# Three moves in the order of a relational graph layer: a maximum's transposes, one pair's input, two gathers of gate rows

## The chip, the cores and the metric

The kernel runs on one core of a Trainium2 chip. The metric is the device time of one execution in microseconds, as the median of several runs. The profile is of one further execution, taken by the hardware profiler; its times are counted from the first instruction.

The core's engines are TensorE (PE; PEld is its weight load), VectorE (DVE), ScalarE (ACT), GpSimd (POOL) and SyncE (SP). Each works through its own instructions in program order. SP, ACT and POOL also issue DMAs. L204 is line 204 of the kernel.

## The reference

One pre-normed graph layer over 1250 nodes of 1024 features, with 20000 typed edges and 8 relations, all in float32:

```python
h = maximum(layernorm(x), 0)
u = h @ root + bias
for r in range(8):
    mask = (edge_type == r)
    sums = segment_sum(h[src] * mask[:, None], dst, num_segments=1250)
    cnt  = segment_sum(mask, dst, num_segments=1250)
    u = u + (sums / maximum(cnt, 1)[:, None]) @ weight[r]
z = concatenate([u, h], axis=1) @ w_gate + b_gate
out = x + tanh(u) * z + h * (1 - z)
```

## The kernel before, in words

**Matrices before edges.** The kernel multiplies h by each of the eight relation matrices first and gathers rows of the products afterwards. There are eleven matrices in all, numbered 0 to 10: the relations, root (8), the lower half of w_gate (9), and the upper half (10), which multiplies u. The nodes are ten blocks of 128 rows, taken in five pairs: pair i holds blocks i and i + 5. We write (s, i) for the product of matrix s with pair i. There are 55 of them, and their order fixes TensorE's order.

**A product.** One product (`product`, L195) multiplies 256 x 1024 by 1024 x 1024 in seven products of quarters, of four 128-deep steps each. We call these the seven adds, j = 0 to 6, in the order A11, S1, S2, S4, S3, A12, A22. Their left operands lie in `h_op[i]`, seven slices of 512 columns; `transposed` (L174) makes the four A slices by TensorE transposes and copies, `left` (L186) the S slices on VectorE (S1 on L189). Their right operands are the quarters of the matrix and four sums of them that VectorE makes (`make_t1` to `make_t4`, L158 to L172); T4 belongs to A22. An add takes about 3.43 us on TensorE. ScalarE and VectorE take the results out of PSUM: L213, L216, L219, L226 and L234 on ScalarE, L222, L227 and L231 on VectorE. Six PSUM banks are shared.

**Slots.** After each add the kernel calls `between(j)`. This is where all other work is put into the engines' orders: generators are advanced, and whatever stands between two of their `yield`s falls behind that add. We call such a piece a slot and count from the first add of the kernel, or of the stage concerned.

**First stage (products (0,0) to (3,3)).** `norms` normalises the pairs, stores h (`store`, L410) to `h_dram`, transposes it (`factored`), and stores x + h (`with_x`, L414 and L415) to `xh_dram`. `both` is the norm of a pair's two blocks: statistics on VectorE (L388), a square root on ScalarE, and the scaled relu on ScalarE (L405). Pairs 0 and 1 are loaded ahead of the first product. The x tiles come from a pool of three; pair 1's two lie in a part of `h_op[3]` that is not used yet. In `norms`, pair 2 is normalised in slot 8, pair 3 in slot 12, and pair 4 block by block in slots 16 and 18. Beside it, `columns` makes key columns from the edge lists, and later slots count and place the edges in a table and order the nodes by their number of edges.

**Edges.** The relations form three groups, matrices 0 to 2, 3 to 5, and 6 to 7. For each group and each block of nodes, a row of u gathers its edges' rows of the product, one edge per node and slot: an indirect DMA on POOL (L834) into one of four `got` tiles, and a multiply and add on VectorE (L842). Between blocks and groups u lies in `u_dram`, written by L308 and read by L302. The second group's slots, 76 of them, lie beside the products of matrices 6 and 7 (70 adds).

**Passes.** Nodes with more edges than the slots provide need further passes, whose number is computed at run time. `passes_needed` (L901) takes maxima on VectorE (L908 and L910) in its first step and then transposes them on TensorE (L914 and L915). A few small VectorE instructions (L917 to L925) turn them into `n_pass`, which every engine reads before the branch at L974, at the end of the second group. `with_passes` advances this generator once per slot of the second group.

**The gate.** The last matrix runs pair by pair in the order of the sorted nodes. `gate_u` gathers h rows, takes tanh of u and makes the left operand of the next product. `gate_load` loads u (`last_dram`) and gathers root rows (`hr_dram`), added on L1042, for the pair after the next. `gate_rows` gathers rows of `z_dram` and `xh_dram` and multiplies them on L1078. `finish` forms the output. For pair 0 the z rows go to `h_op[2]`; `z_dram` is written by the SP stores of matrix 9 (L277). All gathers are issued by POOL in program order.

Of the kernel before, what the change touches and what calls it, by code (L numbers as in the profile page):

```python
# [9 lines left out]
F32 = mybir.dt.float32  # L10
# [9 lines left out]
def tile_rgcn_highway(  # L20
# [34 lines left out]
    P = 128  # L55
    N, D = x.shape
# [6 lines left out]
    NP = ND // 2  # L63
# [16 lines left out]
    A11, A12, A22, S1, S2, S3, S4 = range(7)  # L80
# [23 lines left out]
    z_dram = dram.tile([N, D], F32, name="z_dram")  # L104
    xh_dram = dram.tile([N, D], F32, name="xh_dram")
# [68 lines left out]
    def transposed(aop, part, of, n):  # L174

        for half, to in enumerate(((A11, A12), (A21, A22))[part]):
            p = bank().rearrange("p (k f) -> p k f", k=KQ)
            for i in range(KQ):
                k = KQ * half + i
                nc.tensor.transpose(p[:, i, :n], of[:n, k * P:(k + 1) * P], ident[:n, :n])  # L180
            copy = nc.vector.tensor_copy if half else nc.scalar.copy
            copy(aop[:, to, :, :n], p[:, :, :n])
            if n < P:
                nc.gpsimd.memset(aop[:, to, :, n:], 0.0)

    def left(aop, part=0):  # L186

        if part != 3:
            nc.vector.tensor_add(aop[:, S1], aop[:, A21], aop[:, A22])  # L189
            nc.vector.tensor_sub(aop[:, S2], aop[:, S1], aop[:, A11])  # L190
        if part != 1:
            nc.vector.tensor_sub(aop[:, S4], aop[:, A12], aop[:, S2])
            nc.vector.tensor_sub(aop[:, S3], aop[:, A11], aop[:, A21])
# [94 lines left out]
    node = const.tile([P, G, ND], I32, name="node")  # L288
# [9 lines left out]
    h_op = [keep.tile([P, 7, KQ, P], F32, name=f"h_op{i}") for i in range(NP)]  # L298

    def rows_of(to, of, at):  # L300

        nc.gpsimd.indirect_dma_start(  # L302
            out=to, out_offset=None, in_=of,
            in_offset=bass.IndirectOffsetOnAxis(ap=at, axis=0))
# [52 lines left out]
    with ExitStack() as early:  # L357
# [4 lines left out]
        xpool = first_part.enter_context(tc.tile_pool(name="xpool", bufs=3))  # L362

        def load_x(i, part, t=None):
            d = i + part * NP
            n = nrows(d)
            if t is None:
                t = xpool.tile([P, D], F32, name="xt")
            nc.sync.dma_start(t[:n], x[d * P:d * P + n, :])
            return t  # L370

        def scratch(i, part):

            return h_op[i][:, 2 * part:2 * part + 2].rearrange("p a k f -> p (a k f)")
# [42 lines left out]
        def both(a, b, parts=1):  # L417

            a.stats(0)
            a.stats(1)  # L420
            a.spread()
            b.stats(0)
            a.scale()
            a.relu(parts)
            b.stats(1)
            b.spread()
            b.scale()
            b.relu(parts)

        def factored(i, blocks):  # L430
            for part in range(2):
                transposed(h_op[i], part, blocks[part].ht, blocks[part].n)
# [7 lines left out]
        x1 = [load_x(1, 0, scratch(NP - 2, 0))]  # L440
        fac[0].load_b21()
        x1.append(load_x(1, 1, scratch(NP - 2, 1)))
        xs = [load_x(2, 0)]


        ix0 = first_part.enter_context(tc.tile_pool(name="ix0", bufs=1))
# [288 lines left out]
        def norms():  # L735
            yield
            yield
            both(*b1)
            fac[0].make_t4()
            for b in b1:  # L740
                b.store()
            yield
            yield
            factored(1, b1)
            left(h_op[1])
            yield
            for b in b0:
                b.with_x()
            xs.extend([load_x(2, 1), load_x(3, 0)])
            yield  # L750
            for b in b1:
                b.with_x()
            yield
            yield
            for i in range(2, NP):
                blocks = []
                if i < NP - 1:
                    blocks = [Normed(i + part * NP, xs.pop(0), scratch(NP - 1, part))
                              for part in range(2)]
                    both(*blocks)  # L760
                    yield
                    for b in blocks:
                        b.store()
                    yield
                    factored(i, blocks)
                    left(h_op[i])
                    yield
                    for b in blocks:
                        b.with_x()
                    xs.append(load_x(i + 1, 1))  # L770
                    if i + 2 < NP:
                        xs.append(load_x(i + 2, 0))
                    yield
                else:
                    for part in range(2):
                        xt = xs.pop(0)
                        b = Normed(i + part * NP, xt, xpool.tile([P, D], F32, name="xt"))
                        b.stats(0)
                        b.stats(1)
                        b.spread()  # L780
                        b.scale()
                        b.relu()
                        b.store()
                        yield
                        transposed(h_op[i], part, b.ht, b.n)
                        b.with_x()
                        yield
                    left(h_op[i])
            first_part.close()

        def index():
# [17 lines left out]
    with ExitStack() as edges_part:  # L809
# [91 lines left out]
        def passes_needed():  # L901

            far_k = small.tile([P, NHI], F32, name="far_k")
            nc.vector.memset(far_k, 0.0)
            for g in range(G):
                for d in range(ND):
                    if K[g][d] < SLOTS:
                        nc.vector.reduce_max(far_k[:, g * ND + d:g * ND + d + 1],  # L908
                                             w_of[:, g, d, K[g][d]:], axis=AX.X)
            nc.vector.reduce_max(most[:, 1:2], far_k, axis=AX.X)  # L910
            for _ in range(3):
                yield
            p = bank()
            nc.tensor.transpose(p[:1, :P], most[:, 0:1], ident)  # L914
            nc.tensor.transpose(p[:1, P:2 * P], most[:, 1:2], ident)  # L915
            top = const.tile([1, 2], F32, name="top")
            nc.vector.reduce_max(top, p[:1, :2 * P].rearrange("o (a b) -> o a b", a=2), axis=AX.X)  # L917
            nc.vector.tensor_scalar(top[:, 0:1], top[:, 0:1], float(MORE - 1 - SLOTS), 0.0,
                                    op0=OP.add, op1=OP.max)
            nc.vector.tensor_single_scalar(top[:, 1:2], top[:, 1:2], 0.0, op=OP.is_gt)  # L920
            top_i = const.tile([1, 2], I32, name="top_i")
            nc.vector.tensor_copy(top_i, top)
            nc.vector.tensor_single_scalar(top_i[:, 0:1], top_i[:, 0:1], 2,
                                           op=OP.arith_shift_right)
            nc.vector.tensor_max(n_pass, top_i[:, 0:1], top_i[:, 1:2])  # L925
# [10 lines left out]
        s, i = next(steps)  # L936
        while s <= R0[1]:
            step(s, i)
            s, i = next(steps)
# [8 lines left out]
        def with_others(e):  # L948
# [6 lines left out]
            for _ in others:  # L955
# [3 lines left out]
        s, i = beside(with_others(edges(0, range(ND), u_back(0))), sum(K[0]) + 1, s, i,  # L959
                      R0[2] - 1)  # L960
# [6 lines left out]
        for g in range(1, G - 1):  # L967
            e = edges(g, range(ND), u_back(g))
            s, i = beside(with_passes(e) if g == G - 2 else e, sum(K[g]) + 1, s, i, R0[g + 2] - 1)
# [4 lines left out]
        with tc.If(passes > 0):  # L974
# [15 lines left out]
            scratch = got()  # L990
# [14 lines left out]
            with tc.For_i(0, passes, 1):  # L1005
# [9 lines left out]
                for c in range(NCH):  # L1015
                    n = nedges(c)
# [13 lines left out]
        LG = G - 1  # L1030
# [17 lines left out]
        def place_of(what, i, part):  # L1048

            o = ("z", "d").index(what)  # L1050
            if i % 2:
                w = fac[NM - 1].spare[o].rearrange("p k n -> p (k n)")
                return w[:, part * D:(part + 1) * D]
            return h_op[2 + o][:, 2 * part:2 * part + 2].rearrange("p a k f -> p (a k f)")

        def pair(i):
            return [(part, 2 * i + part, nrows(2 * i + part)) for part in range(2)]

        hs, xhs, adds, outs = {}, {}, [], []
# [7 lines left out]
        def gate_rows(i, j):  # L1067

            if j == 0:
                for part, d, n in pair(i):  # L1070
                    at = node[:n, LG, d:d + 1]
                    rows_of(place_of("z", i, part)[:n], z_dram[:, :], at)
                    xhs[part] = got()
                    rows_of(xhs[part][:n], xh_dram[:, :], at)
            elif j == (2 if i else 5):
                for part, d, n in pair(i):
                    zt, dt = place_of("z", i, part), place_of("d", i, part)
                    nc.vector.tensor_mul(zt[:n], zt[:n], dt[:n])  # L1078
                    nc.vector.tensor_add(zt[:n], zt[:n], xhs[part][:n])
# [109 lines left out]
```

## Time and profile before

| | us |
|---|---|
| median of 3 runs (lowest, highest) | 1408.04 (1406.12, 1408.88) |
| profiled execution, its own time | 1409.14 |
| its span, first to last instruction | 1407.3 |
| TensorE busy | 1369.7 (97%) |
| VectorE busy | 862.4 (61%) |
| GpSimd busy | 616.8 (44%) |
| ScalarE busy | 339.4 (24%) |
| mean granted TensorE clock | 0.99 |

Busy time counts the instructions of an engine, not its waits. Where an idle time stands in brackets before an instruction, an arrow names what ended it, its releaser. A line of the timeline has a start, a length, the engine, the line of the kernel, the operation, the tiles written and read, and the number of instructions merged into it. DMA-issuing instructions on SP are short; their data moves afterwards.

### The profile page before, as it was taken

The page shows a single profiled execution, that of the slowest core. Times are in us where ns is not written, and L with a number is a line of the kernel's source. Part 1 is how long each engine was busy: PE and PEld are TensorE (multiplying, and loading weights), DVE is VectorE, ACT ScalarE, POOL GpSimd, SP SyncE. Part 2 cuts the span into 40 slices and gives each one's busy share as a digit, 9 for nine tenths or more (in the row PEclk, how much of TensorE's full clock was granted, in tenths as well). Part 3 has the DMA queues.
Part 4 walks back from the last instruction along what each step waited for, and adds up shares of the span by engine and source line. Part 5 has one row for each costly group of instructions (what it writes and reads, how often), then busy time and mean ns, then how long its engine had stood idle before and what let it go on. Part 6 is the DMA issues. An engine that isn't in the chain of part 4 may idle for free.

```text
span 1407.3 us, 11968 instructions
## 1 busy us (share of the span) xinstructions
PE 1369.7 (97%) x3562; PEld 617.4 (44%) x3562; DVE 862.4 (61%) x1658; ACT 339.4 (24%) x721; POOL 616.8 (44%) x567
## 2 busy tenths in 40 slices
PE   7989999999999999999999599999999999999998
PEld 4444444444444444444444244444444444444443
DVE  7755866886767834455456545654446565465985
ACT  3235655565521111011111010111111111121220
POOL 0001655665561634665664434544426433422641
PEclk9999999999999999999999899999999999999999
DMA  9653766675544257269677725787659844556761
GB/s 327 219 191 114 182 119 129 151 194 103 123 134 134 63 180 195 88 199 269 209 279 252 273 89 196 275 305 261 231 171 328 304 161 171 190 188 207 255 234 56
DMA packets 109863, 272.73 MB, mean 194 GB/s; under 512 B 25890, under 2 KB 27920, under 8 KB 109664
## 3 DMA queue, kind: packets, MB, share of 16 engines
q0 software_dynamic: 48864, 128.60, 28.4%
q1 hardware_dynamic: 39808, 101.38, 24.7%
q10 hardware_dynamic: 21120, 41.95, 9.6%
q8 instruction: 28, 0.46, 0.1%
q14 instruction: 43, 0.35, 0.1%
HBM read 214.20 MB, written 80.65 MB: 210 GB/s over the span
## 4 chain that ended last, share of the span: by engine, by line
PE 72%; issue 9%; DMA 6%; POOL 5%; DVE 2%; ACT 0%; POOLq 0%; DVEq 0%; ACTq 0%
PE ps L204 71%; DMA got<-y,idx 3%; DMA node_dram<-ids,pos_i 2%; POOL got L834 2%; POOL got L302 1%; POOL out_dram L308 1%; DMA got<-hr_dram,node 1%; PE ps_n L585 1%; DVE u L842 1%; DMA got<-h_dram,node 1%; POOL u_dram L308 1%; PE ps L180 0%; POOL idx L302 0%; POOL h_op L302 0%; DMA xh_dram<-xt 0%
## 5 line engine op out<-in xcount | busy, mean ns | idle before, releaser
L204 PE MATMUL ps<-w,h_op 128*128 128x512 f32 x3080 | 1347.5, 596 | 2.9 <-DVE h_op L189 2.9
L204 PEld LDWEIGHTS ps<-w,h_op 128*128 128x128 f32 x3080 | 580.3, 191 | 700.3 <-issue 691.9
L842 DVE SCALAR_TENSOR_TENSOR u<-got,w_of,u 128x1024 f32<-128x1024 f32 (+1 forms) x192 | 246.2, 1283 | 197.3 <-DMA got<-y,idx 189.2
L834 POOL DMA_INDIRECT got<-y,idx x202 | 244.8, 1212 | 243.1 <-DVE u L842 163.4
L664 POOL DMA_INDIRECT table<-row_col,at_i x157 | 179.3, 1142 | 159.1 <-DVE at_i L660 65.7
L222 DVE TENSOR_TENSOR row<-row,ps 128x512 f32<-128x512 f32 x55 | 37.7, 685 | 113.3 <-PE ps L204 86.3
L226 ACT COPY part<-ps 128x512 f32<-128x512 f32 x55 | 32.2, 586 | 291.2 <-PE ps L204 282.6
L234 ACT COPY row<-ps 128x512 f32<-128x512 f32 x50 | 29.3, 585 | 253.1 <-PE ps L204 253.1
L213 ACT COPY row<-ps 128x512 f32<-128x512 f32 x55 | 32.1, 585 | 165.0 <-PE ps L204 148.5
L227 DVE TENSOR_TENSOR row<-row,part 128x512 f32<-128x512 f32 x55 | 37.8, 688 | 50.4 <-ACT part L226 44.2
L216 ACT COPY row<-ps 128x512 f32<-128x512 f32 x55 | 32.1, 584 | 144.7 <-PE ps L204 131.8
L219 ACT COPY row<-ps 128x512 f32<-128x512 f32 x55 | 32.1, 584 | 134.3 <-PE ps L204 126.1
L308 POOL DMA_INDIRECT u_dram<-u,node x20 | 29.6, 1480 | 76.6 <-DVE u L842 72.8
L650 DVE SCALAR_TENSOR_TENSOR junk<-k_bc,key_col,before 128x128 f32<-128x128 int32 x157 | 54.9, 350 | 4.2
L339 POOL DMA_INDIRECT node_dram<-ids,pos_i x30 | 35.5, 1183 | 42.3 <-issue 41.5
L590 DVE TENSOR_TENSOR seen<-seen,ps_n 128x110 f32<-128x110 f32 x157 | 42.1, 268 | 15.8 <-PE ps_n L585 11.4
L718 DVE SCALAR_TENSOR_TENSOR junk<-v_bc,val,one 128x1280 bf16<-128x1280 f32 x30 | 46.5, 1550 | 7.4 <-DMA v_bc<-val_dram 6.6
L567 ACT ACTIVATE is_lo<-io,less_lo 128x128 bf16<-128x128 f32 x157 | 50.1, 391 | 0.8 <-DMA xh_dram<-xt 0.8
L231 DVE TENSOR_TENSOR row<-row,ps 128x512 f32<-128x512 f32 x55 | 37.5, 682 | 20.2 <-PE ps L204 17.5
L160 DVE TENSOR_TENSOR w<-w,w 128x2048 f32<-128x2048 f32 x11 | 25.2, 2290 | 30.1 <-PE ps L204 30.1
L302 POOL DMA_INDIRECT u<-u_dram,node x20 | 19.2, 960 | 48.0 <-DMA u_dram<-u,node 33.6
L302 POOL DMA_INDIRECT idx<-table,node_key x30 | 33.8, 1128 | 9.1 <-issue 8.5
(159 smaller groups left out, 715.1 us busy)
## 6 DMA issues: line engine op xcount, KB each, us to landing
y<-row SPq DMA_DIRECT2D x72, 512.0 KB
w<-in_L_gnn_weight_dram ACTq DMA_DIRECT2D x28, 1024.0 KB
k_bc<-keys_dram SPq DMA_DIRECT2D x39, 256.0 KB
l_bc<-los_dram SPq DMA_DIRECT2D x39, 256.0 KB
w<-in_L_gnn_w_gate_dram ACTq DMA_DIRECT2D x8, 1024.0 KB
hr_dram<-row SPq DMA_DIRECT2D x9, 512.0 KB
z_dram<-row SPq DMA_DIRECT2D x9, 512.0 KB
w<-in_L_gnn_weight_dram SPq DMA_DIRECT2D x4, 1024.0 KB
```

The source lines that it names most:

```text
L204: nc.tensor.matmul(b, aop[:, i, k, :], w.of[i][:, k, :], start=(fresh and k == 0), stop=(k == KQ - 1), skip_group_check=True)
L222: nc.vector.tensor_add(c12, c12, c)
L227: nc.vector.tensor_add(c22, c22, d)
L302: nc.gpsimd.indirect_dma_start(out=to, out_offset=None, in_=of, in_offset=bass.IndirectOffsetOnAxis(ap=at, axis=0))
L308: ins = nc.gpsimd.indirect_dma_start(out=of, out_offset=bass.IndirectOffsetOnAxis(ap=at, axis=0), in_=frm, in_offset=None)
L567: nc.scalar.activation(is_lo[:, i, :], io, AF.Abs, bias=less_lo[:, c0 + i:c0 + i + 1])
L590: nc.vector.tensor_add(seen[j][:, i, :], was, p[:, i, :])
L650: nc.vector.scalar_tensor_tensor(junk, o["k_bc"][:, i, :], key_col[:, c:c + 1], before, op0=OP.is_equal, op1=OP.mult, accum_out=rank[:, c: ...
L664: ins = nc.gpsimd.indirect_dma_start(out=table[:, :], out_offset=bass.IndirectOffsetOnAxis(ap=at_i[:n, i:i + 1], axis=0), in_=row_col[:n, ...
L718: nc.vector.scalar_tensor_tensor(junk, v_bc[:, g, :], val[:, c:c + 1], one.to_broadcast([P, KEYS]), op0=OP.is_gt, op1=OP.mult, accum_out=p ...
L834: nc.gpsimd.indirect_dma_start(out=t[:n], out_offset=None, in_=y[g][:, :], in_offset=bass.IndirectOffsetOnAxis(ap=at[:n, d, k:k + 1], axis=0),
L842: nc.vector.scalar_tensor_tensor(u[:n], t[:n], w, u[:n], op0=OP.mult, op1=OP.add)
```

## The change

It has three parts.

**A.** The generator `passes_needed` yields 30 times instead of three between the maxima and their transposes. The transposes, the small instructions behind them and `n_pass` move from slot 3 to slot 30 of the second group.

**B.** The `norms` generator is written out without its loop, in another order. Both halves of pair 2's x are loaded ahead of the first product, the first of them into the slices S1 and S2 of `h_op[2]`. Both halves of pair 3's x are loaded in slot 5. The norms of pair 2 move from slot 8 to 5, its transposes from slot 10 to 8, the norms of pair 3 from 12 to 10 with transposes from 14 to 12, and pair 4's blocks from 16 and 18 to 14 and 16. `with_x` of pair 2 comes ahead of its `left` and that of pair 1 moves from slot 6 to 7. The generator ends two slots earlier.

**C.** For the first pair of the gate product, the two gathers of z rows move from behind the first add (j = 0) to behind the fourth (j = 3). The two xh gathers stay. For the other pairs the z gathers come behind the xh gathers of the same slot, where they alternated with them before.

```diff
-        xs = [load_x(2, 0)]
+        x2 = [load_x(2, 0, h_op[2][:, S1:S2 + 1].rearrange("p a k f -> p (a k f)")), load_x(2, 1)]
...
             for b in b0:
                 b.with_x()
-            xs.extend([load_x(2, 1), load_x(3, 0)])
+            x3 = [load_x(3, part) for part in range(2)]
+            b2 = [Normed(2 + part * NP, x2[part], scratch(NP - 1, part)) for part in range(2)]
+            both(*b2)
+            yield
+            for b in b2:
+                b.store()
             yield
             for b in b1:
                 b.with_x()
             yield
-            yield
-            for i in range(2, NP):
-                blocks = []
-                if i < NP - 1:
-                    blocks = [Normed(i + part * NP, xs.pop(0), scratch(NP - 1, part))
-                              for part in range(2)]
-                    both(*blocks)
-                    yield
-                    for b in blocks:
-                        b.store()
-                    yield
-                    factored(i, blocks)
-                    left(h_op[i])
-                    yield
-                    for b in blocks:
-                        b.with_x()
-                    xs.append(load_x(i + 1, 1))
-                    if i + 2 < NP:
-                        xs.append(load_x(i + 2, 0))
-                    yield
...
+            factored(2, b2)
+            for b in b2:
+                b.with_x()
+            left(h_op[2])
+            x4 = [load_x(4, 0)]
+            yield
+            yield
+            b3 = [Normed(3 + part * NP, x3[part], scratch(NP - 1, part)) for part in range(2)]
+            both(*b3)
+            yield
+            for b in b3:
+                b.store()
+            yield
+            factored(3, b3)
+            left(h_op[3])
+            yield
+            for b in b3:
+                b.with_x()
+            x4.append(load_x(4, 1))
+            yield
...
-            for _ in range(3):
+            for _ in range(30):
                 yield
             p = bank()
             nc.tensor.transpose(p[:1, :P], most[:, 0:1], ident)
...
             if j == 0:
                 for part, d, n in pair(i):
-                    at = node[:n, LG, d:d + 1]
-                    rows_of(place_of("z", i, part)[:n], z_dram[:, :], at)
                     xhs[part] = got()
-                    rows_of(xhs[part][:n], xh_dram[:, :], at)
+                    rows_of(xhs[part][:n], xh_dram[:, :], node[:n, LG, d:d + 1])
+            if j == (0 if i else 3):
+                for part, d, n in pair(i):
+                    rows_of(place_of("z", i, part)[:n], z_dram[:, :], node[:n, LG, d:d + 1])
             elif j == (2 if i else 5):
```

## The prediction

> **What bounds the kernel now.** I read the page's busy line, then TensorE's waits, then the timelines of all engines around each wait. From the page:
>
> ```profile
> PE 1369.7 (97%) x3562; PEld 617.4 (44%) x3562; DVE 862.4 (61%) x1658; ACT 339.4 (24%) x721; POOL 616.8 (44%) x567
> ```
>
> TensorE is busy 1369.7 of 1407.3 us; a change of order can win at most the other 37.6. Its waits (line, releaser, total us, times, longest):
>
> ```profile
> PE ps L915 <- DVE most L910: 14.4, 1, 14.4
> PE ps L180 <- ACT h_op L405: 10.9, 3, 7.6
> PE ps L204 <- DVE h_op L189: 2.9, 2, 2.8
> PE ps L180 <- ACT xt L405: 2.2, 2, 1.4
> ```
>
> 7.6 us of the second row is the start, before x has arrived, and 6.9 us lie behind the last matmul (1400.4 to 1407.3); the change touches neither. Left are 14.4 at L915, 3.3 + 2.2 at the early transposes and 2.8 late. With start and tail that makes 37.2, nearly all of the 37.6. Each part of the change aims at one of these waits.
>
> The first, in TensorE's timeline (start, length, instruction, idle before) and then VectorE's:
>
> ```profile
> 777.74 0.27 PE L914 MATMUL ps<-ident,most 128*1 128x128 f32 x1
> 792.44 0.37 PE L915 MATMUL ps<-ident,most 128*1 128x128 f32 x1 [14.43 <-DVE most L910]
> ```
> ```profile
> 788.63 1.28 DVE L842 SCALAR_TENSOR_TENSOR u<-got,w_of,u 128x1024 f32<-128x1024 f32 x1 [13.10 <-DMA got<-y,idx]
> 789.99 2.18 DVE L908 TENSOR_REDUCE far_k<-w_of 128x1 f32<-128x10 f32 x28
> 792.20 0.18 DVE L910 TENSOR_REDUCE most<-far_k 128x1 f32<-128x30 f32 x1
> ```
>
> VectorE stands 13.1 us for the second group's first gather. The reductions are behind it in its order, so the transposes, three slots on in TensorE's order, stop TensorE.
>
> The early ones, on TensorE, with VectorE's wait before them:
>
> ```profile
> 70.90 1.09 PE L180 MATMUL ps<-ident,h_op 128*128 128x128 f32 x8 [2.50 <-ACT h_op L405]
> 72.80 1.86 PE L180 MATMUL ps<-ident,h_op 128*128 128x128 f32 x8 [0.81 <-ACT h_op L405]
> 86.66 1.09 PE L180 MATMUL ps<-ident,xt 128*128 128x128 f32 x8 [0.79 <-ACT xt L405]
> 96.07 0.89 PE L180 MATMUL ps<-ident,xt 98*128 98x98 f32 x8 [1.45 <-ACT xt L405]
> ```
> ```profile
> 68.57 0.69 DVE L388 BATCH_NORM_STATS2 st<-xt 128x6 f32<-128x512 f32 x1 [3.75 <-DMA xt<-in_x_dram]
> ```
>
> The second half of pair 3's x is issued at 64.4 and wanted by VectorE at 64.8.
>
> The late one, on GpSimd, VectorE and TensorE:
>
> ```profile
> 1279.75 0.95 POOL L302 DMA_INDIRECT h_op<-z_dram,node  x1 [17.39 <-issue]
> ```
> ```profile
> 1293.85 2.46 DVE L1042 TENSOR_TENSOR u<-u,got 128x1024 f32<-128x1024 f32 x2 [17.10 <-DMA got<-hr_dram,node]
> ```
> ```profile
> 1298.96 13.63 PE L204 MATMUL ps<-w,h_op 128*128 128x512 f32 x24 [2.77 <-DVE h_op L189]
> ```
>
> GpSimd stands at the z gather until the last z rows, issued at 1273.4, are in memory. The xh and hr gathers queue behind it, hr at 1284.8 and 1286.0; VectorE waits for hr and makes the next left operand 2.77 us late.
>
> **What the Trainium skill says.** "Perfetto Trace Analysis", section "Optimization Strategy": find the gaps on the engine that matters and what it waits for there. The sum of gaps above agrees. "DMA: Bandwidth & Descriptors", section "Anatomy of one DMA — SWDGE (gpsimd) path": about 2.0 us plus bytes over 436 GB/s, an estimate of 3.2 us for 512 KB. It is fitted for GpSimd's path; here SP's stores of xt rows took 2.7 us (61.7 until the load that needed the buffer, 64.4) and 4.7 us (80.5 to 85.2). The same page, "Issuing engines are not separate DMA queues": all queues share the 16 engines, so an added early load delays what is behind it. The trace moves 400 to 410 GB/s from 3 to 20 us.
>
> **Part A, the transposes of the maximum 27 slots later.** Nothing is added: two transposes (0.27 and 0.37 us) and six small VectorE instructions (L917 to L925, 796.14 to 797.4, 1.3 us) move. The reductions stay in slot 0. The 76 slots lie beside 70 adds (two matrices x 5 products x 7), so slot 30 falls at the 28th add, the end of product (6,3). At 3.43 us per add that is some 866 us, 74 us after the reductions end at 792.4. TensorE no longer waits there: **14.4 us**.
>
> What is late next? TensorE runs 14.4 us further ahead of VectorE. VectorE still stands until 788.6, is through reductions and three slots at 796.1 and then owes L222 of (6,0), ready since 781.3. TensorE needs that bank and those rows only two products later, after 815. VectorE catches up before: between 796 and 847 it waited for TensorE's results 0.9 + 2.1 + 0.9 + 7.6 + 2.1 + 9.0 = 22.6 us, more than 14.4. The last of these:
>
> ```profile
> 846.73 0.69 DVE L222 TENSOR_TENSOR row<-row,ps 128x512 f32<-128x512 f32 x1 [9.00 <-PE ps L204]
> ```
>
> So the first block's scatter (848.9) stays paced by TensorE and the chain of gathers behind it shifts along. That matters, because from 906 on this chain is paced by its own gathers, and at its end there is no slack: T4 of matrix 8 stands behind it.
>
> ```profile
> 1042.81 2.29 DVE L172 TENSOR_TENSOR w<-w,w 128x2048 f32<-128x2048 f32 x1 [6.05 <-DVEq L974]
> ```
>
> It is finished at 1045.1, and TensorE's add A22 of (8,0), which reads T4, starts at 1045.2. I put the cost there at 0; the bounds are 0 and all 14.4, if the chain did not shift. The moved 1.3 us on VectorE falls where it waited 5.9 us (before 887.5). n_pass is needed at 1018, 150 us later.
>
> **Part B, the order of the first 100 us.** No arithmetic is added. On SP, pair 2's second x moves into the preamble (at 8.6 us, 512 KB, 1.3 us at 400 GB/s ahead of edge lists needed at 40), pair 3's second x from slot 11 to 5; all norms of pair 2 on move two or three slots up, with their stores. One wait is added: pair 2's first x lies in S1 and S2 of h_op[2], so S1 (L189) must wait on VectorE for its store to xh_dram.
>
> VectorE by the old rows: with_x of pair 0 ends 37.4; both norms of pair 2 take 4.1 (44.7 to 48.8), 41.5; casts 2.4, 43.9; with_x of pair 1 2.3, 46.2; rows and tb 2.6, 48.8; two copies 1.4, 50.2; with_x of pair 2 2.3, 52.5. Its first store goes out at 51.4 and, at 2.7 to 4.7 us, lands at 54.1 to 56.1; I take 55, since y and xh stores are ahead of it. left 2.7, key columns 0.8, L222 0.6: pair 3's norms start at 59.1, and the relus end 3.6 and 5.5 later, 62.7 and 64.6. TensorE: add 8 ends 44.5, transposes 1.8, add 9, columns 1.2, adds 10 to 12, 61.3. It waits 1.4 and 1.1 for the two relus, 2.5 against 3.3. ScalarE's L226, queued behind these relus, ends at 65.1, before add 13 needs it. So the wait for the load becomes a smaller wait for VectorE's backlog: 0.8 won. Block 4 keeps its 0.8 (the same distance between norms and transposes). Block 9 no longer stands behind an L227 that waits for TensorE: its norms start near 81, its relu ends near 85.2, the transposes come at 86.3: 1.45 won. **B: 2.3 us**; bounds 5.5 won, and 3 lost if the store lands 5 us later, each us of landing being one of TensorE.
>
> **Part C, two z gathers from add 0 to add 3.** They pass two xh, two hr and two h gathers. The xh and hr buffers are free from 1268 to 1272, so hr goes out near 1274 instead of 1285; with 4 MB of other traffic hr and the u rows land near 1282, VectorE adds until 1284.5, and S1 is ready near 1287, nine us before TensorE asks (1296.2). **2.8 us.** The z rows go out near 1288 behind the h gathers and land near 1295; the multiply that reads them ran at 1304.5. If they were later they would delay VectorE's finish, which has two products of room. Bounds 0 to 2.8.
>
> **Sum.** 14.4 + 2.3 + 2.8 = 19.5. The profiled execution took 1409.1 us (span 1407.3 and 1.8 around it): 1389.6. The median of the runs, 1408.0, is 1.1 lower: **1388.5**.
>
> **Rivals.**
> 1. The gain of A is given back: VectorE does not catch up, T4 of matrix 8 is late and TensorE stands at A22 of (8,0). The zero slack at 1045 speaks for it, the 22.6 us against it. Fully returned: 1408.0 − 5.1 = 1402.9; half: 1396. Chance 0.09.
> 2. B loses: the new store wait or the fuller SP queue costs 1 to 5 us net instead of winning 2.3, giving 1392 to 1396. Chance 0.15.
> 3. Slower: the wait at L189 for pair 2's store. Everything on VectorE stands behind it, and pair 3's relus on ScalarE with L226 behind them, so TensorE stands as long. To eat 19.5 us the store must land later than about 75 us, 23 us after issue; the longest seen is 4.7. Beyond that the total passes 1408. Chance, with all unnamed ways to slower, 0.05.
> 4. The change does nothing at L915 because the reductions wait for something else; they do not, all but the gather ahead of them is in the rows above. Chance 0.02, at 1403, no loss.
>
> The main forecast has the remaining 0.69, 1386 to 1391. All waits gone would give 1408.0 − 22.7 = 1385.3, so the range ends at 1384.5 below; above, it takes in rival 2 and the milder half of rival 1, 1395. Faster than before by over 0.2% (about what a measurement here tells from no change, 2.8 us): 0.93; within: 0.02; slower: 0.05.
>
> **What would show it.** Right: no L915 in TensorE's waits; no L189 wait near 1280; about 2.5 us left at L180 for pair 3 and none at the last transposes; a VectorE wait at L189 for the xh_dram store of 1.5 to 3.5 us near 53; TensorE's busy time unchanged. Wrong: a TensorE wait at L204 released by L172 (rival 1), or L180 waits above 6 us in the first 100 (rival 2).

## The result, and the profile after

| | before | after |
|---|---|---|
| median of 6 runs (lowest, highest), us | 1408.46 (1406.12, 1409.77) | 1383.62 (1383.08, 1385.41) |
| profiled execution, us | 1409.14 | 1385.41 |
| span, us | 1407.3 | 1383.6 |
| TensorE busy, us | 1369.7 | 1364.6 |

The ratio is 0.9826, 95% interval 0.9814 to 0.9839: 24.8 us faster. The forecast was 1388.5, 19.5 faster, with a range from 1384.5 to 1395.0. The direction was right; the time fell 0.9 us below the range.

The page after, part 1, and TensorE's waits:

```profile
PE 1364.6 (99%) x3562; PEld 615.9 (45%) x3562; DVE 861.1 (62%) x1658; ACT 339.4 (25%) x721; POOL 630.1 (46%) x567
```
```profile
PE ps L180 <- ACT h_op L405: 11.5, 3, 7.6
PE ps L204 <- DVE w L172: 0.4, 1, 0.4
```

The wait at L915 is gone, and so is the late one at L189. The waits add up to 11.9 us where they were 30.4 before: 18.5 less, near the 19.5 forecast. But the spans of the profiled executions are 23.7 us apart. The rest is in the first line: the same 3562 instructions keep TensorE busy 5.1 us less. The prediction had this figure unchanged.

The transposes of the maximum, now on L917 and L918, no longer stand:

```profile
862.43 0.27 PE L917 MATMUL ps<-ident,most 128*1 128x128 f32 x1
862.54 0.27 PE L918 MATMUL ps<-ident,most 128*1 128x128 f32 x1
```

Part B's stretch, VectorE at the added wait and then TensorE:

```profile
56.56 0.69 DVE L189 TENSOR_TENSOR h_op<-h_op 128x512 f32<-128x512 f32 x1 [4.07 <-DMA xh_dram<-h_op]
60.50 1.28 DVE L388 BATCH_NORM_STATS2 st<-xt 128x6 f32<-128x512 f32 x2
```
```profile
64.22 1.09 PE L180 MATMUL ps<-ident,h_op 128*128 128x128 f32 x8 [3.10 <-ACT h_op L405]
66.12 1.97 PE L180 MATMUL ps<-ident,h_op 128*128 128x128 f32 x8 [0.81 <-ACT h_op L405]
67.88 12.61 PE L204 MATMUL ps<-w,h_op 128*128 128x512 f32 x24
80.33 1.04 PE L180 MATMUL ps<-ident,xt 128*128 128x128 f32 x8
88.07 0.84 PE L180 MATMUL ps<-ident,xt 98*128 98x98 f32 x8
```

The store took 5.2 us from VectorE's last use of the tile (51.3) to its release (56.5); the estimate was 3.6. Pair 3's transposes wait 3.9 us in all, and the three adds behind them take 12.6 us. At the full clock they take 10.5 (10.47 in late_left below). Blocks 4 and 9 no longer wait.

Part C's stretch, on VectorE:

```profile
1267.09 1.22 DVE L1045 TENSOR_TENSOR u<-u,got 128x1024 f32<-128x1024 f32 x1 [7.59 <-DMA got<-hr_dram,node]
1271.74 0.69 DVE L189 TENSOR_TENSOR h_op<-h_op 128x512 f32<-128x512 f32 x1
```

VectorE waits 7.6 us for the hr rows instead of 17.1, and S1 is there before TensorE asks for it.

### The profile page after: what moved, and what is told of

Its sections match the earlier page's. It is cut to its first block, busy times and chain, and to the rows that moved or that the text cites. A ratio compares the mean times of both kernels' runs of the same rounds, so it can differ in the third digit from the quotient of the medians.

```text
span 1383.6 us, 11973 instructions
## 1 busy us (share of the span) xinstructions
PE 1364.6 (99%) x3562; PEld 615.9 (45%) x3562; DVE 861.1 (62%) x1658; ACT 339.4 (25%) x721; POOL 630.1 (46%) x567
## 5 line engine op out<-in xcount | busy, mean ns | idle before, releaser
L837 POOL DMA_INDIRECT got<-y,idx x202 | 249.3, 1234 | 230.7 <-DVE u L845 140.7
L226 ACT COPY part<-ps 128x512 f32<-128x512 f32 x55 | 32.2, 585 | 269.5 <-PE ps L204 269.5
```

Source lines behind the costliest of these rows:

```text
L837: nc.gpsimd.indirect_dma_start(out=t[:n], out_offset=None, in_=y[g][:, :], in_offset=bass.IndirectOffsetOnAxis(ap=at[:n, d, k:k + 1], axis=0),
```

## The experiments

The first question was where the excess over the forecast comes from (4.2 us between the two profiles, 5.3 between the medians). Theory 1: a wait on TensorE costs more than its length, because the matmuls behind it run at a lower granted clock. Theory 2, the prediction's accounting: a wait costs its length. Theory 3 came after the first runs: the waits of the one profiled execution were not the usual ones.

**The three parts alone.** Each is one part of the diff on the kernel before; b_only is the changed kernel with `range(3)` and the old order of the z gathers.

> Part A alone on the kernel before. Theory 1 (a TensorE wait costs its length and then some microseconds of matmuls at half the granted clock): 14.4 us of wait at L915 plus 1.9 us of slow matmuls behind it (13.8 us at a granted 0.86) go, so 16.3 us less than before, some 1392. Theory 2 (a wait costs its length alone, as the prediction reckoned): 14.4 less, some 1394. Both: TensorE's wait for L172 is 0.5 us or less.

> Part B alone on the kernel before. In the changed kernel the waits at L180 in the first 100 us fell from 5.5 to 3.9 us, but the three adds behind pair 3's transposes took 12.6 us instead of 11.4. Theory 1: 1.6 won and 1.2 lost again at the low clock, 0 to 1 us less than before. Theory 2: 1.6 us less. The prediction had 2.3. A theory in which B brings the unexplained 5 us would need 6 us or more here.

> Part C alone on the kernel before. Theory 1: the wait of 2.8 us goes and the three adds behind it take 10.3 us instead of 13.6, so 6.1 us less than before. Theory 2: 2.8 us less.

| | median, us | before on this chip | ratio, 95% interval | difference, us |
|---|---|---|---|---|
| a_only | 1390.25 | 1410.27 | 0.9857, 0.9833 to 0.9882 | −20 |
| b_only | 1410.48 | 1410.27 | 1.0006, 0.9993 to 1.0019 | +1 |
| c_only | 1403.41 | 1410.27 | 0.9953, 0.9932 to 0.9974 | −7 |

The differences are the ratios times 1410. A wins more than either theory gave: its interval is 16.6 to 23.5 us, and the 16.3 of theory 1 lies just below it. C wins what theory 1 gave (interval 3.7 to 9.6, without the 2.8 of theory 2), B nothing. The traces add something neither theory had. B and C don't touch the wait at L915, and yet it is longer there than 14.4 us, in c_only and b_only:

```profile
PE ps L915 <- DVE most L910: 20.7, 1, 20.7
```
```profile
PE ps L918 <- DVE most L913: 17.8, 1, 17.8
```

**The kernel before, profiled again (theory 3).**

> The kernel before, unchanged, profiled again. Theory 3 (the wait at L915 differs from execution to execution, and the 14.4 us of the first profile were at the short end): a wait between 14 and 21 us there, as in the kernels with B alone (17.8) and C alone (20.7), which don't touch it, and a time that follows it. Against it: 14.4 again to 0.5 us, so that the longer waits would be the doing of B and C.

> The same once more, for a third value: theory 3 expects one that differs from the other two by a microsecond or more; otherwise 14.4 again.

TensorE's waits in before_2, and the line for L915 in before_3:

```profile
PE ps L915 <- DVE most L910: 21.6, 1, 21.6
PE ps L180 <- ACT h_op L405: 10.1, 3, 7.4
PE ps L180 <- DVE row L1140: 3.1, 1, 3.1
PE ps L204 <- DVE h_op L189: 2.9, 1, 2.9
PE ps L180 <- ACT xt L405: 2.0, 2, 1.5
```
```profile
PE ps L915 <- DVE most L910: 15.8, 1, 15.8
```

14.4, 15.8 and 21.6 us at L915, in executions of 1409.1, 1407.0 and 1414.9 us: theory 3 holds for the wait. The time follows it only in part: before_3 is 2.1 us faster than the first profile with a wait 1.4 us longer, because it gains 2.0 us in the first stage and 1.4 in C's stretch (the table of stretches further down). What differs is ahead of the first gather. GpSimd issues the second group's first gather of u rows only when the first group's last scatter to `u_dram` has landed. This is GpSimd's timeline in the first profile and in before_2:

```profile
773.63 2.76 POOL L308 DMA_INDIRECT u_dram<-u,node  x1 [5.74 <-DVE u L842]
779.58 0.99 POOL L302 DMA_INDIRECT u<-u_dram,node  x1 [3.20 <-DMA u_dram<-u,node]
```
```profile
776.38 2.76 POOL L308 DMA_INDIRECT u_dram<-u,node  x1 [5.75 <-DVE u L842]
786.01 1.00 POOL L302 DMA_INDIRECT u<-u_dram,node  x1 [6.88 <-DMA u_dram<-u,node]
```

The scatter started 2.8 us later and kept GpSimd 3.7 us longer, while TensorE, which does not depend on it until L915, was there 2.8 us earlier (774.9 against 777.7). That is 9.3 us against the 7.2 between the two waits; the other 2.1 us came back on the way from the gather to L915. The other traces with the wait fit: GpSimd stands 3.6 us for this landing in before_3, 6.7 in b_only and 7.9 in c_only, where the waits at L915 are 15.8, 17.8 and 20.7. Why the landing varies, no run here tells.

The third line of before_2 is a wait that the first profile does not have. TensorE's timeline of before_2 shows where it stands:

```profile
1303.06 10.57 PE L204 MATMUL ps<-w,h_op 128*128 128x512 f32 x24 [2.87 <-DVE h_op L189]
1313.46 1.47 PE L180 MATMUL ps<-ident,u 128*128 128x128 f32 x12
1318.06 0.66 PE L180 MATMUL ps<-ident,u 128*128 128x128 f32 x4 [3.13 <-DVE row L1140]
```

Behind the late left operand stands a second obstacle. The next transposes need a PSUM bank that still holds the last result of (10,0). VectorE, late for the same hr rows, takes it with L1140 only at 1317.3. In the first profile this second wait was hidden: the three adds ahead of it took 13.63 us instead of 10.57, at a low clock, so the transposes came late enough by themselves. From the start of one pair's transposes to the next TensorE took 31.9 us there (1280.5 to 1312.4) and 25.8 us in the changed kernel (1263.3 to 1289.1). So C is worth 6.1 us in these two profiles, of which the prediction had counted 2.8. Theory 1's 6.1 us for C is this same sum. In a_only, before_2 and before_3 the three adds ran at the full clock (10.57 us), and the wait at L1140 stood in the open (3.3, 3.1 and 3.0 us).

**A wait filled with work.** In the kernel before, ahead of the transposes:

```diff
+            q = bank()
+            for _ in range(15):
+                nc.tensor.matmul(q, ident, h_op[0][:, A11].rearrange("p k f -> p (k f)"),
+                                 start=True, stop=True)
             p = bank()
```

> The kernel before, with 15 matmuls of 128x512 (12.9 us, their result unused) ahead of the two transposes of the maximum, so that TensorE works through most of the wait at L915 and idles some 1.5 us of it. The wait still ends when VectorE is done. Theory 1: the granted clock stays at 1.00 behind it and 1.9 us are won against before, although work was added. Theory 2: no change, 0 us.

Median 1408.15 us, ratio 0.9986 (0.9974 to 0.9999): 2.0 us faster, as theory 1 said, in an interval from 0.1 to 3.7. It is weak evidence: the wait ran long in the profiled execution, 3.15 us were left of it, and the low clock followed all the same (a granted 0.59 from 793 to 797). The runs that follow measure the price by itself.

**Made waits.** In the changed kernel, ten times, with n copies:

```diff
+            if s in (4, 5) and j == 4:
+                for _ in range(n):
+                    nc.scalar.copy(ident, ident)
+                p = bank()
+                nc.tensor.transpose(p[:, :P], ident, ident)
             between(j)
```

> The changed kernel with ten made waits on TensorE, one in each product of matrices 4 and 5: behind the fifth add ScalarE copies a 128x128 tile onto itself once and TensorE transposes it (result unused), so TensorE waits about 1.0 us each time, for nothing else. Both theories, length alone (2) and length plus low clock (1): 13 us more than the changed kernel, ten times 1.0 and a transpose of 0.27.

> Ten made waits with four copies each. One copy gave a wait of 0.87 us, nine gave 3.51, so four give about 1.9. If the low clock needs a wait of about 3 us or more, 21 to 22 us more than the changed kernel (1.9 and 0.2 for the transpose, ten times); if any wait brings it, 2 us each more, 40.

> The same with nine copies: ten waits of about 3.4 us. Theory 2 (length alone): 37 us more than the changed kernel. Theory 1 (low granted clock behind a wait of some 3 us): 1 to 3 us more for each, 47 to 67 us in all, and a granted clock well below 1.00 behind the waits in the trace.

> Ten made waits with 18 copies each, some 6.5 us. If what follows a wait is a fixed time at the low clock, 2.7 us each as behind the waits of 3.5, or less where the clock comes back by chance: 6.5 + 0.3 + 2 to 3, ten times, 88 to 98 us more than the changed kernel. If the loss grows with the wait, more than 110.

The changed kernel took 1385.2 us on the chip of stall1 and stall9. The other two ran on a chip where it was not measured; for them I take 1384.5, the mean of its three medians (1383.6, 1385.2, 1384.6).

| copies | wait each, us | median, us | more than the changed kernel | per wait | seven adds behind a wait |
|---|---|---|---|---|---|
| 1 | 0.87 | 1395.92 | 10.7 | 1.1 | |
| 4 | 1.86 | 1406.15 | 21.6 | 2.2 | 24.2 |
| 9 | 3.51 | 1450.47 | 65.2 | 6.5 | 26.9 |
| 18 | 6.47 | 1474.87 | 90.4 | 9.0 | 25.5 to 27.0 |

TensorE in stall4 and in stall9 (the waits follow one another in the same form):

```profile
569.14 0.33 PE L266 MATMUL ps<-ident 128*128 128x128 f32 x1 [1.86 <-ACT ident L264]
569.30 24.20 PE L204 MATMUL ps<-w,h_op 128*128 128x512 f32 x56
```
```profile
577.70 0.48 PE L266 MATMUL ps<-ident 128*128 128x128 f32 x1 [3.51 <-ACT ident L264]
577.97 26.88 PE L204 MATMUL ps<-w,h_op 128*128 128x512 f32 x56
```

Theory 1 holds for the longer waits. Waits of 0.87 and 1.86 us cost their length and the transpose, 0.2 or 0.3 us (with one copy 10.7 us in all, where 13 was expected from a wait of 1.0). A wait of 3.51 us costs 3.0 more, of which 2.7 are in the seven adds behind it. The loss does not grow with the wait: at 6.47 us it is 2.5. The windows of stall9 (length, TensorE busy, granted clock, DMA share, GB/s) show the clock:

```profile
547.00:551.00 4.00, 3.91 (x6) 0.50 1.09 244
551.00:555.00 4.00, 4.00 (x8) 0.79 0.53 195
555.00:574.00 19.00, 19.00 (x45) 1.00 0.25 73
```

The Trainium skill, "TensorE: Matmul & The Clock Gate", section "What's actually happening", says that the clock falls to half after an idle window of about 3.4 us and comes back after a busy one, and that these windows run freely. The traces agree with the free windows. In the clock records of the 17 traces every stretch at the low clock ahead of the last matmul lasts 3.41 us or a multiple of it (13.65 at L915 in the first profile), and within one trace all of them begin and end on one grid of that step. But the window need not be idle, and a wait that is shorter than the window can bring the low clock. Here are windows of the grid around the late left operand (same columns), in the first profile and in before_2:

```profile
1294.93:1298.34 3.41, 1.25 (x3) 1.00 0.17 26
1298.34:1301.75 3.41, 2.79 (x4) 0.50 0.88 292
1301.75:1305.17 3.42, 3.42 (x6) 0.50 0.35 143
1305.17:1308.58 3.41, 3.41 (x10) 1.00 0.67 196
```
```profile
1298.27:1301.69 3.42, 1.92 (x5) 1.00 0.03 12
1301.69:1305.10 3.41, 2.04 (x5) 1.00 0.88 259
1305.10:1308.51 3.41, 3.41 (x9) 1.00 0.54 202
```

The wait of 2.77 us fell mostly into one window and left 1.25 us of work in it; two windows at half the clock followed, and the adds took 3.1 us longer. In before_2 the 2.87 us fell across two windows, which kept 1.92 and 2.04 us of work, and nothing followed. The other traces show the same. The clock fell 41 times ahead of the last matmul, 20 of them behind the made waits of stall9 and stall18. In 40 of the 41 TensorE had been busy for at most 1.46 us of the window before, in one for 1.60. No window with less than 1.46 us of work kept the full clock.

This explains the table. A wait of 1.86 us leaves at least 3.41 − 1.86 = 1.55 us of work in any window, just above the 1.46, and none of the ten brought the low clock. The falls in stall9 are 30.72 us apart, nine windows, so its ten waits all met the grid at nearly the same place (0.95 to 1.18 us of work in the window before). They are one case repeated and not ten; what 3.51 us cost at other places of the grid was not measured. A low window full of work costs half its length, 1.7 us: behind the wait at L1140 in a_only, seven adds took 25.88 us instead of 24.20.

**All three parts together, and what spends B.**

> The changed kernel once more, beside the kernel before on this chip. If the parts add up, it is faster than before by the sum of the three parts alone: A 20.0, C 6.6, B about 0, together some 26 us, 1384. If the parts need each other for the excess over 19.5, it is faster by less or more than that sum. Its runs should lie closer together (2 to 3 us) than those of the kernel before (14 us), if the spread of before comes from the wait at L915.

> Parts A and C without B, beside the whole change on the same chip. B alone measured nothing (ratio 1.0006), but there the wait at L915 stood behind it and could take back what was won in the first 100 us. If B wins its 1 to 2 us once A is in, this kernel is 1 to 2 us slower than the whole change; if B is worth nothing in itself, the two agree to 1 us; if B's store wait costs, this one is faster.

> The whole change, as the measure for the other two of this call: 1383 to 1386.

after_again: 1385.24 us, ratio 0.9833 (0.9810 to 0.9856), some 23.5 us faster than the kernel before there (1407.8; interval 20.3 to 26.7), which agrees with the sum of the parts alone (26, where A and C have some 3 us of doubt each). Its runs lie within 2.2 us, those of before within 7.2 there and 14 on the chip of the three parts. Each of the seven sets of 5 or 6 such runs with part A lies within 0.9 to 4.1 us, each without it within 3.7 to 14 (6 to 45 runs). This fits the wait at L915 as the main cause of the spread. ac, on another chip: 1383.76 us; after_3: 1384.56, with runs that overlap (1383.05 to 1385.72 and 1383.54 to 1385.40). B is worth nothing here too, so it is not the wait at L915 that takes its gain.

The traces show each part in its own stretch. ScalarE runs L226 once in each product, so the start of the n-th L226 dates the n-th product:

| stretch, us | without the part | with it |
|---|---|---|
| A: 30th to 34th | 113.0, 119.7, 114.0 (before, 2, 3), 116.9 (b_only), 119.1 (c_only) | 96.1 to 96.6, seven traces |
| B: start to 20th | 520.4, 517.6, 518.4 (before, 2, 3), 518.6 (a_only), 517.3 (c_only), 518.3 (ac) | 518.7 (b_only), 519.3, 519.5, 517.6 (after, again, 3) |
| C: 50th to 53rd | 83.9, 85.6, 82.5 (before, 2, 3), 85.9 (a_only), 83.5 (b_only) | 77.4, seven traces |

A wins 17 to 24 us where it acts and C 5 to 8.5; for B no gain shows even before the 20th product. In the two profiles of the prediction and the result this makes 16.9 + 1.1 + 6.5, and 0.8 is lost between, of the 23.7. The first profile was also the slowest of six without B at the 20th product, so B was priced from an execution with a slow start.

To test the added store wait I moved one line of the changed kernel:

```diff
             for b in b2:
                 b.with_x()
-            left(h_op[2])
...
             both(*b3)
+            left(h_op[2])
```

> The changed kernel with pair 3's norms ahead of left of pair 2 on VectorE, so that VectorE no longer stands 4.1 us at L189 ahead of these norms. If that wait is what makes pair 3's transposes late, TensorE's waits there (3.1 and 0.8 us) go, and with them 2.3 us of matmuls at the low clock: 4 to 6 us less than the changed kernel, about 1378. If the transposes are late for VectorE's other work, 0 to 1 us less.

> The changed kernel with left of pair 2 behind the norms of pair 3, again and in one call with the kernel without B: 4 us less than the whole change, as before. If B with this order beats A and C alone, the order of the first 100 us was worth something and only the store wait spent it.

Medians 1381.36 us (the changed kernel 1385.24 beside it) and 1382.64 us (1384.56 beside it, ac 1383.76): 3.9 and 1.9 us faster than the change, in runs that do not overlap with it, and the fastest kernel on both chips. Its lead over ac is 1.1 us, in runs that overlap a little. In late_left and late_left_2 the 20th product comes at 515.2 and 516.1 us, earlier than in all traces of the table: B's order is worth something once `left` stands behind these norms. The move takes `left`'s own 2.7 us of work away from ahead of the norms together with the 4.1 us of wait, so the runs do not separate the two. In late_left VectorE reaches pair 3's norms at 55.6 instead of 60.5. Its waits on TensorE:

```profile
PE ps L180 <- ACT h_op L405: 7.4, 1, 7.4
PE ps L180 <- ACT xt L405: 2.4, 1, 2.4
```

Only the start is left of the first line: pair 3's waits are gone. Block 4 now waits 2.4 us, since its relu writes into a tile whose x + h store has not landed. The forecast of 4 to 6 us missed this next wait. 3.9 us came of it, and 1.9 where 4 was expected again. In late_left_2's trace the wait of 2.35 us fell into one window (1.06 us of work left), and the 16 matmuls behind its transposes took 7.96 us at the low clock; in late_left they took 7.03 behind a wait of 2.36.

## Why the prediction was right or wrong, point by point

- **What bounds the kernel, and which waits go:** right in the main. The first and the third of the named waits went, and nothing came in their place but 0.4 us at L172. The early ones fell from 5.5 to 3.9 us, where 3.2 was forecast. The sum of waits that went, 18.5 us against 19.5, is close partly by luck: the longest of them was near its shortest in the profile from which it was read.
- **Part A, TensorE running ahead:** right in mechanism. VectorE caught up, and T4 of matrix 8, named as the place without slack, cost 0.4 us after the change, 0.3 in ac, and nothing in after_again.
- **Part A, its size: the step that failed most.** The term "14.4 us" was the wait's length in one execution. Three profiles of the same kernel have 14.4 to 21.6, and some 1.9 us of low clock come on top (13.8 us at a granted 0.86 behind the wait in the first profile). Alone it measured 20.
- **Part C, its size: less than half of what it won.** The term "2.8 us" stopped at the first wait. A second stood behind it, the bank that L1140 frees late, and the low clock hid it in the profile: 6.1 us in the traces, 7 measured. The sentence that VectorE's finish has two products of room was wrong for this bank: it is wanted within one product.
- **Part B:** the last two transposes lost their waits, one more than forecast. But the store landed 1.5 us later than estimated: VectorE stood 4.1 us at L189, where 1.5 to 3.5 was forecast, and TensorE 3.9 us at pair 3, where 2.5 was. The low clock came behind it (12.6 us for three adds). "2.3 us" measured as nothing, once alone and once beside A and C. The 5.5 us it set out from was one execution's as well: the five other traces with the old order have 4.4 to 5.3. One reading is off without weight: the 400 to 410 GB/s from 3 to 20 us are 373 to 413.
- **"TensorE's busy time unchanged", and the floor of 1385.3:** wrong. Busy time contains the matmuls at the low clock. Half of the busy time in the low windows is 6.9 us before and 3.0 after, which is 3.9 of the 5.1; the other 1.2 is not traced. The floor subtracted only waits, and so did "at most the other 37.6" at the start; the lower end of the range stood on it.
- **The rivals:** none came true. The nearest was the second: B won nothing, but no loss shows; the range failed on the other side, where there was no rival at all for a gain larger than the sum of the waits.

## What to carry to other kernels

A wait on a busy TensorE is priced as its length plus the matmuls at the low clock behind it. In these traces the made waits of up to 1.86 us brought none, and between 2.35 and 3.3 us it depended on where the wait fell. Look at the granted clock and the length of the same adds right behind each gap. Before a gap's length goes into a sum, look for the next thing that the late engine owes TensorE, which may stand hidden behind the slow matmuls. And a wait that ends on a DMA's landing differs from one execution to the next: profile the kernel before more than once, or give that term a range.

## What the hardware showed that was not expected

- The step in the price of a wait: 1.86 us cost 2.2, 3.51 us cost 6.5, and 6.47 us cost 9.0, each averaged over ten.
- What makes the step: in these traces the clock fell to half behind a window of 3.41 us in which TensorE had less than about 1.5 us of work. The window need not be idle. So a wait of 2.77 us brought it in one execution, and 2.87 us at the same place in another did not.
- The landing of one and the same scatter to `u_dram` (2.76 us of issue in both) kept GpSimd standing 3.2 us in one execution of the kernel before and 6.9 us in another. With it moved the wait at L915: 14.4, 15.8 and 21.6 us in three executions.
